# Biases of two projections from one group of two-column products, and a new order for the first two pairs of a four-layer transformer-like kernel

## The chip, the cores and the metric

The kernel runs on one core of a Trainium2 chip. The metric is the device time of one execution in microseconds (us), start to end. The engines are named as the profile names them: PE is TensorE (PEld its weight loads), DVE is VectorE, ACT is ScalarE, POOL is GpSimd, and SP is SyncE, which here only issues DMAs. All data is 32-bit floating point.

## The reference, cut to what matters

There are 32 samples; each has x and f (256 positions by 256 features). Four residual layers follow each other:

```python
x = x + attention(x, f, seq_len)      # 16 heads of 16; keys and values from x, one more from f itself
x = x + adapter(x, language_id)       # two small products, then a normalisation
x = x + (x @ W[subject].T + b[subject])
x = x + pool(x, prompt_type)          # tanh scores, masked softmax over positions
```

In the attention the queries and the keys have biases that are added to the inputs ahead of the projection:

```python
query = f + b_self
key   = concatenate([x + b_prev, f + b_self])
q = query @ Wq + bq
k = key @ Wk + bk
```

The kernel folds each of these into one bias per output feature, computed once: `b_self @ Wq + bq` for the queries, `b_prev @ Wk + bk` for the keys of x, and `b_self @ Wk + bk` for the keys of f.

## The kernel before, in words

The samples go through in 16 pairs. Every pair is cut into some 200 steps, each a small function that issues a few instructions on one or two engines. No loop nest sets the order: tables give every step of a pair a place (a number), places of pair p are shifted by 16 for each pair, all steps of all pairs are sorted by place, and the instructions are issued in that order. Engines run their own instructions strictly in that order; waits between engines are semaphores. One table (`SLOTS`) serves the pairs 2 to 13, so that the steps of three to four pairs interleave the same way again and again; `FIRST` and `SECOND` hold the places of the pairs 0 and 1, two more tables those of the last two pairs, and `ONCE` those of the setup steps. So the order can differ between two kernels in the start alone and be the same for the rest.

The steps that matter here, with their lines:

- **Idle products** (`setup_warm`, L1236): two products of a constant 128x256 tile into a PSUM tile that nobody reads. They keep PE running. `setup_warm(n)` for n from 0 to 4 are five groups of them.
- **Bias products** (`shifted`, L1246): four products of 128x128 weights with one column each. `setup_q` (tile bq_ps), `setup_k` (bk_ps) and `setup_ks` (bks_ps) each issue one such group, then a few tiny operations of DVE. They need `bcols_in` and the weights `wks` or `wqs`.
- **Projections** (`proj_q`, `proj_k`, `proj_ks`, L1542): four rows of PE in the trace each, into qps, kps and ksps; `proj_v` and `self_values` (L1409) into v_ps and vs_ps.
- **First scores** (`s1`, L1646): keys as the moving operand, so that `row_max` (L1659, DVE, into nmpad) can take the maximum over keys of four heads at a time. All s1 tiles but four share one PSUM buffer: the next s1 can't start until `row_max` of the one before has read it.
- **Second scores** (`s2`, L1757): the same products transposed, into one other PSUM buffer, which `exps` (L1769, ACT) empties. The next s2 waits for that.
- s1 and s2 use 32 rows of the PE array per head, and `g` says which half of the rows. An s1 and an s2 of different halves that are neighbours in the queue run side by side.
- `max_T` (nm_ps, L1677), `own` (own_ps, L1597), `av` (L1779), `vs`, `tw_ps` (L1448) and the other products fill the time between two s1.

In what follows s1(b,n,g) is the s1 step of sample b (b = 2 x pair + i).

Of the kernel before, what the change touches and what calls it, by code (L numbers as in the profile page):

```python
# [36 lines left out]
    (("setup_warm", 3), -134.4553),  # L37
    (("setup_heads",), -117.1977),
    (("setup_load", "wk"), -107.6222),
    (("setup_warm", 2), -106.4704),  # L40
    (("setup_warm", 4), -100.8478),
    (("setup_len",), -86.8814),
    (("setup_load", "wq"), -85.6382),
    (("setup_ks",), -80.858),
    (("setup_load", "lang"), -58.21),
    (("setup_warm", 1), -46.8993),
    (("setup_ones",), -45.2227),
    (("setup_k",), -44.8904),
    (("setup_load", "wv"), -39.5338),
    (("setup_load", "bo"), -39.016),  # L50
    (("setup_load", "subj"), -36.5512),
    (("setup_load", "wo"), -33.8195),
    (("setup_q",), -32.6784),
    (("setup_tw_load", 0), -28.6522),
    (("setup_warm", 0), -17.3426),
    (("setup_load", "ptype"), -16.0265),
    (("setup_xconst",), -14.8955),
    (("setup_mcol",), -4.8071),
    (("setup_load", "pw"), -2.9408),
    (("setup_tw_load", 1), -2.291),  # L60
    (("setup_tw_bias",), 3.0863),
    (("setup_tw", 0), 4.4234),
    (("setup_tw_load", 2), 6.8896),
    (("setup_tw", 1), 7.7073),
    (("setup_tw_load", 4), 10.7892),
    (("setup_tw", 2), 13.4697),
    (("setup_tw_load", 3), 15.8592),
    (("setup_tw", 3), 19.3226),
    (("setup_tw", 4), 20.7528),
    (("setup_tw_load", 5), 22.4043),  # L70
    (("setup_pool",), 22.7791),
    (("setup_tw", 5), 24.2208),
    (("setup_tw_load", 6), 26.6611),
    (("setup_tw", 6), 27.4389),
    (("setup_vbc",), 34.3784),
    (("setup_tw_load", 7), 37.2938),
    (("setup_tw", 7), 40.4841),
# [207 lines left out]
    (("load_T", "xT"), -71.3129),  # L285
    (("key_mask", 0), -56.3002),
    (("mask_keys", 0), -50.461),
    (("load_T", "fT"), -49.4222),
    (("key_mask", 1), -46.3901),
    (("proj_q", 0), -28.2207),  # L290
    (("q_out", 0), -19.4412),
    (("proj_ks", 0), -17.1577),
    (("spread_q", 0, 0), -17.0194),
    (("mask_keys", 1), -16.4653),
    (("proj_q", 1), -15.9679),
    (("load_x",), -15.7202),
    (("spread_q", 0, 1), -15.5783),
    (("ks_out", 0), -15.5433),
    (("q_out", 1), -14.7452),
    (("proj_k", 0), -10.9121),  # L300
    (("proj_ks", 1), -10.3247),
    (("k_out", 0, 0), -9.1406),
    (("ks_out", 1), -8.2877),
    (("proj_v", 0), -7.7128),
    (("k_out", 0, 1), -6.3829),
    (("v_out", 0), -4.6066),
    (("s1", 0, 0, 1), -2.8235),
    (("s1", 0, 0, 0), -0.5535),
    (("proj_k", 1), -0.4229),
    (("row_max", 0, 0, 0), 0.4669),  # L310
    (("row_max", 0, 0, 1), 0.884),
    (("k_out", 1, 1), 2.0272),
    (("s1", 0, 1, 0), 2.8899),
    (("row_max", 0, 1, 0), 3.0595),
    (("self_values", 0), 3.1147),
    (("s1", 0, 1, 1), 3.3786),
    (("k_out", 1, 0), 3.8795),
    (("s1", 0, 2, 0), 4.0777),
    (("row_max", 0, 2, 0), 4.1575),
    (("row_max", 0, 1, 1), 4.238),  # L320
    (("vs_blocks", 0), 4.4602),
    (("s1", 0, 3, 0), 5.238),
    (("s1", 0, 2, 1), 5.4565),
    (("row_max", 0, 3, 0), 6.7563),
    (("s1", 1, 0, 0), 6.76),
    (("row_max", 0, 2, 1), 7.3706),
    (("s1", 0, 3, 1), 7.4376),
    (("spread_q", 1, 1), 7.6485),
    (("row_max", 1, 0, 0), 7.661),
    (("own",), 9.3522),  # L330
    (("row_max", 0, 3, 1), 9.5492),
    (("s1", 1, 0, 1), 10.0423),
    (("row_max", 1, 0, 1), 10.3329),
    (("max_T", 0), 10.3569),
    (("ones_rows", 0), 10.3914),
    (("own_out",), 10.7488),
    (("spread_q", 1, 0), 10.7762),
    (("s1", 1, 1, 0), 11.3645),
    (("max_own", 0), 11.5999),
    (("own_exp", 0), 11.7836),  # L340
    (("row_max", 1, 1, 0), 11.8145),
    (("s1", 1, 1, 1), 12.1572),
    (("s2", 0, 0, 0), 12.2591),
    (("row_max", 1, 1, 1), 12.5264),
    (("s1", 1, 2, 0), 13.2568),
    (("row_max", 1, 2, 0), 13.3839),
    (("exps", 0, 0, 0), 13.4022),
    (("s2", 0, 0, 1), 13.4124),
    (("s1", 1, 2, 1), 13.5948),
    (("exps", 0, 0, 1), 13.714),  # L350
    (("own_blocks", 0), 13.8403),
    (("s2", 0, 1, 0), 13.983),
    (("x_bias",), 14.4585),
    (("exps", 0, 1, 0), 14.7727),
    (("row_max", 1, 2, 1), 15.4798),
    (("proj_v", 1), 15.4854),
    (("s1", 1, 3, 0), 15.5535),
    (("s2", 0, 1, 1), 15.7304),
    (("exps", 0, 1, 1), 15.7305),
    (("weighted", 0), 15.7581),  # L360
    (("row_max", 1, 3, 0), 16.0315),
    (("s1", 1, 3, 1), 16.9468),
    (("s2", 0, 2, 0), 16.9651),
    (("row_max", 1, 3, 1), 17.0407),
    (("av", 0, 0), 17.0447),
    (("av", 0, 1), 17.6199),
    (("exps", 0, 2, 0), 18.4377),
    (("av_blocks", 0, 0), 18.446),
    (("ones_rows", 1), 18.9042),
    (("v_out", 1), 18.968),  # L370
    (("sums", 0, 0), 18.9765),
    (("s2", 0, 2, 1), 18.9799),
    (("max_T", 1), 19.2223),
    (("exps", 0, 2, 1), 19.399),
    (("s2", 0, 3, 0), 19.8184),
    (("exps", 0, 3, 0), 19.8964),
    (("max_own", 1), 19.8964),
    (("av", 0, 2), 20.1287),
    (("s2", 0, 3, 1), 20.2874),
    (("exps", 0, 3, 1), 20.3348),  # L380
    (("own_exp", 1), 20.558),
    (("s2", 1, 0, 0), 21.0468),
    (("av", 0, 3), 21.6144),
    (("exps", 1, 0, 0), 21.7231),
    (("with_own", 0, 0), 21.8227),
    (("s2", 1, 0, 1), 22.1821),
    (("exps", 1, 0, 1), 22.2235),
    (("self_values", 1), 22.3238),
    (("av_blocks", 0, 1), 22.5492),
    (("vs_blocks", 1), 22.7345),  # L390
    (("s2", 1, 1, 0), 23.1936),
    (("sums", 0, 1), 23.6381),
    (("exps", 1, 1, 0), 23.8054),
    (("s2", 1, 1, 1), 23.9013),
    (("av", 1, 0), 24.0492),
    (("exps", 1, 1, 1), 24.5088),
    (("with_own", 0, 1), 24.7647),
    (("s2", 1, 2, 0), 25.0826),
    (("exps", 1, 2, 0), 25.1529),
    (("av", 1, 1), 25.3201),  # L400
    (("av_blocks", 1, 0), 25.5849),
    (("att_T", 0), 25.7719),
    (("s2", 1, 3, 0), 25.7801),
    (("own_blocks", 1), 25.8013),
    (("exps", 1, 3, 0), 26.1089),
    (("out_proj", 0), 26.2623),
    (("x1_out", 0), 26.4979),
    (("s2", 1, 2, 1), 26.5221),
    (("weighted", 1), 26.6676),
    (("exps", 1, 2, 1), 27.3647),  # L410
    (("load_adapter", 0), 27.443),
    (("blocks", 0, "x1"), 27.6156),
    (("s2", 1, 3, 1), 27.8925),
    (("av", 1, 2), 28.1614),
    (("exps", 1, 3, 1), 28.4053),
    (("av", 1, 3), 29.02),
    (("sums", 1, 0), 29.1336),
    (("with_own", 1, 0), 29.1947),
    (("av_blocks", 1, 1), 29.6903),
    (("load_adapter", 1), 29.7913),  # L420
    (("sums", 1, 1), 30.082),
    (("x1_b2", 0), 30.1782),
    (("with_own", 1, 1), 30.7119),
    (("to_dram", 0, "x1"), 30.7583),
    (("att_T", 1), 31.1704),
    (("load_pool",), 31.5326),
    (("out_proj", 1), 31.5501),
    (("x1_out", 1), 31.6749),
    (("x1_beta", 1), 31.6866),
    (("blocks", 1, "x1"), 31.7378),  # L430
    (("to_dram", 1, "x1"), 32.1915),
    (("from_dram", 0, "x1"), 32.74),
    (("from_dram", 1, "x1"), 33.1075),
    (("hidden",), 33.6373),
    (("x1_b2", 1), 34.2189),
    (("h_out",), 35.1321),
    (("adapted",), 35.3561),
    (("y_out", 1), 35.67),
    (("y_out", 0), 35.8418),
    (("norm_stats", 0), 36.4135),  # L440
    (("norm_rstd", 0), 36.4274),
    (("norm_stats", 1), 36.9029),
    (("norm_rstd", 1), 38.0777),
    (("norm_shift", 0), 38.1002),
    (("norm_shift", 1), 38.1822),
    (("norm", 1), 38.8884),
    (("x1_beta", 0), 39.4462),
    (("x2_out", 1), 39.4886),
    (("load_subject",), 40.5689),
    (("blocks", 1, "x2"), 41.1393),  # L450
    (("norm", 0), 41.7146),
    (("x2_out", 0), 42.754),
    (("to_dram", 1, "x2"), 44.1278),
# [637 lines left out]
def cond_resid_kernel(  # L1091
# [43 lines left out]
    def g_tile(name):  # L1135
        return ps_g.tile([P, 512], F32, tag="g", name=name)
# [1027 lines left out]
```

## Time and profile before

| | |
|---|---|
| median of 3 runs | 1030.31 us (1029.19 to 1030.33) |
| the profiled execution | 1031.86 us, its span from first to last instruction 1030.1 us |
| PE busy | 1017.4 us, 99% of the span |
| DVE, ACT, POOL busy | 77%, 50%, 36% |
| granted PE clock, mean over the span | 0.994 of full speed |

The span leaves 1.8 us around it. PE rows: one product of 32-bit data shows as two rows ("x8" is four products). Ends of PE rows are modelled and include the time in which a product drains, so that a busy PE is not a PE without pauses. The chain of work that ended last is better for pauses: it follows each instruction back to what released it.

### The profile page before, as it was taken

Reading aid. Unit: us, or ns where it says so; the run is one execution under the profiler, and the core shown is the slowest. Engines: PE = TensorE matmul, PEld = TensorE weight load, DVE = VectorE, ACT = ScalarE, POOL = GpSimd, SP = SyncE. Lnnn points to the kernel's source line nnn. Section 1 sums busy time; section 2 is a strip of 40 time slices with the busy share of each in tenths; the row PEclk is TensorE's granted clock in tenths of the full one; section 3 lists DMA queues with packets and bytes.
Section 4 is the critical chain, followed back from the end, with each engine's and each line's share of the span. In section 5 each row is a group of like instructions: output and inputs, shape, how many; then the busy total and the mean of one; then the engine's idle time right before and its main releaser. Section 6 shows DMA issues by size and latency. Waiting matters only on the chain.

```text
span 1030.1 us, 21215 instructions
## 1 busy us (share of the span) xinstructions
PE 1017.4 (99%) x7612; PEld 616.4 (60%) x7612; DVE 793.5 (77%) x1419; ACT 510.1 (50%) x798; POOL 366.1 (36%) x490
## 2 busy tenths in 40 slices
PE   9999999999999999999999999999999999999997
PEld 6466555665656656565665656556565665656565
DVE  4666686878878878787888878787887878877674
ACT  2344454546455555544645454455545455554552
POOL 3014334333334324343333334333333433342461
PEclk9999999999999999999999999999999999999999
DMA  4123334534656454464635536463454645445341
GB/s 172 28 70 113 84 113 124 135 102 113 175 121 171 99 136 126 101 165 118 169 92 136 142 95 171 115 170 88 131 161 107 150 113 143 117 107 129 81 116 61
DMA packets 205487, 125.18 MB, mean 122 GB/s; under 512 B 128646, under 2 KB 176518, under 8 KB 205382
## 3 DMA queue, kind: packets, MB, share of 16 engines
q1 hardware_dynamic: 204854, 122.25, 44.9%
q8 instruction: 60, 0.98, 0.4%
q10 hardware_dynamic: 288, 0.79, 0.2%
q0 software_dynamic: 240, 0.79, 0.2%
q14 instruction: 45, 0.37, 0.1%
HBM read 90.47 MB, written 31.73 MB: 119 GB/s over the span
## 4 chain that ended last, share of the span: by engine, by line
PE 97%; DVE 1%; ACT 1%; issue 1%; POOL 0%; DVEq 0%; ACTq 0%; POOLq 0%
PE s L1646 16%; PE s L1757 12%; PE av L1779 11%; PE qps L1542 6%; PE vs_ps L1409 6%; PE v_ps L1409 6%; PE o_ps L1409 6%; PE kps L1542 6%; PE p_ps L1409 6%; PE ksps L1542 6%; PE z_ps L1409 6%; PE y_ps L1890 2%; PE t_ps L1973 2%; PE h_ps L1864 2%; PE sc_ps L2001 1%; PE nm_ps L1677 1%
## 5 line engine op out<-in xcount | busy, mean ns | idle before, releaser
L1769 ACT ACTIVATE e<-s 128x1024 f32<-128x1024 f32 x256 | 261.5, 1023 | 329.7 <-PE s L1757 228.8
L1659 DVE TENSOR_REDUCE nmpad<-s 128x4 f32<-128x1024 f32 x256 | 310.4, 1214 | 93.8 <-PE s L1757 65.7
L1646 PE MATMUL s<-k,qc 32*128 32x512 f32 x1024 | 284.4, 639 | 2.1 <-DVE nmpad L1659 2.0
L1757 PE MATMUL s<-q,k 32*128 32x256 f32 x2048 | 285.6, 400 | 0.9 <-ACT e L1769 0.8
L1757 PEld LDWEIGHTS s<-q,k 32*128 32x128 f32 x2048 | 172.6, 184 | 23.7 <-ACT e L1769 8.1
L1646 PEld LDWEIGHTS s<-k,qc 32*128 32x128 f32 x1024 | 75.9, 183 | 117.3 <-issue 28.4
L1779 PE MATMUL av<-e,vpad 128*32 128x256 f32 x2048 | 130.5, 383 | 0.1
L1810 POOL TENSOR_TENSOR vs<-bt,vs 128x256 f32<-128x256 f32 x64 | 51.9, 811 | 208.3 <-DVE bt L1791 199.0
L1779 PEld LDWEIGHTS av<-e,vpad 128*32 128x32 f32 x2048 | 58.2, 109 | 58.8 <-issue 28.1
L1569 ACT ACTIVATE k<-kps,kbias,cols 128x512 f32<-128x512 f32 x64 | 46.8, 774 | 60.0 <-PE kps L1542 55.2
L1811 POOL TENSOR_TENSOR vs<-vs,zs 128x256 f32<-128x256 f32 x64 | 40.4, 631 | 96.3 <-DVE zs L1801 93.2
L1855 POOL TENSOR_TENSOR x1b<-x,an 128x512 f32<-128x512 f32 x32 | 40.7, 1273 | 80.5 <-DVE x L1834 75.1
L1542 PE MATMUL qps<-fT,wqs 128*128 128x512 f32 x128 | 65.1, 633 | 0.1
L1916 POOL TENSOR_SCALAR rstd<-mv 128x2 f32<-128x2 f32 x32 | 7.5, 235 | 162.0 <-DVE mv L1909 162.0
L1409 PE MATMUL p_ps<-x2b,prT 128*128 128x256 f32 x256 | 63.9, 394 | 0.4 <-DVE pz L2030 0.4
L1409 PE MATMUL v_ps<-wvs,xT 128*128 128x256 f32 x256 | 63.6, 391 | 0.6 <-ACT vpad L1622 0.6
L1409 PE MATMUL vs_ps<-fT,wvs 128*128 128x256 f32 x256 | 63.8, 392 | 0.0
L1409 PE MATMUL o_ps<-wos,attT 128*128 128x256 f32 x256 | 63.4, 390 | 0.0
L1409 PE MATMUL z_ps<-ws,x2T 128*128 128x256 f32 x256 | 62.5, 387 | 0.0
L1542 PE MATMUL kps<-xT,wks 128*128 128x512 f32 x128 | 62.3, 609 | 0.0
L1542 PE MATMUL ksps<-fT,wks 128*128 128x512 f32 x128 | 61.9, 606 | 0.0
L1409 PEld LDWEIGHTS p_ps<-x2b,prT 128*128 128x128 f32 x256 | 48.1, 194 | 17.2 <-issue 11.6
(138 smaller groups left out, 1461.2 us busy)
## 6 DMA issues: line engine op xcount, KB each, us to landing
an<-in_adn SPq DMA_DIRECT2D x32, 384.0 KB
mk<-pool_d SPq DMA_DIRECT2D x32, 257.0 KB
fT<-in_fT SPq DMA_DIRECT2D x16, 512.0 KB
xs<-in_x SPq DMA_DIRECT2D x32, 256.0 KB
ws<-in_swT SPq DMA_DIRECT2D x32, 256.0 KB
out<-x2b SPq DMA_DIRECT2D x32, 256.0 KB
xT<-in_xT SPq DMA_DIRECT2D x15, 512.0 KB
swap_d<-x1bl SPq DMA_DIRECT2D x112, 64.0 KB
```

Of the source, the lines that this page charges most:

```text
L1409: nc.tensor.matmul(ps[:, q, :n], lhsT=lhsT(c, q), rhs=rhs[:, c, :], start=(c == 0), stop=(c == 1),)
L1542: nc.tensor.matmul(ps, lhsT=w[:, ci, c * P : (c + 1) * P], rhs=T[src, p][:, ci].rearrange("p b s -> p (b s)"), start=(ci == 0), stop=(ci = ...
L1569: nc.scalar.activation(joint("k", p, work, [P, 2, 2, 2, S])[:, u, c].rearrange("p b s -> p (b s)"), T["kps", p, c], AF.Identity, bias=kbia ...
L1646: nc.tensor.matmul(ps[:, j].rearrange("p (u s) -> p u s", u=2), lhsT=T["qc", p][r, c, i, q * P : (q + 1) * P], rhs=T["k", p][r, :, c, i, : ...
L1659: nc.vector.tensor_reduce(nm_bufs[i][:, q, to : to + 8].rearrange("p (u j) -> p j u", u=2)[:, 2 * g : 2 * g + 2], T.pop(("s1", b, n, g)).r ...
L1757: nc.tensor.matmul(ps[:, j, k, :], lhsT=T["k", p][r, u, c, i, k * P : (k + 1) * P], rhs=T["q", p][r, u, c, i, :], start=True, stop=True,)
L1769: nc.scalar.activation(e, T.pop(("s2", b, n, g)), AF.Exp)
L1779: nc.tensor.matmul(ps[j * HB : (j + 1) * HB, u, :], lhsT=v_bufs[b % 3][:, k, 8 * c + 2 * j + u, :], rhs=e[j // 2][:, j % 2, k, :], start=( ...
L1810: nc.gpsimd.tensor_tensor(vs, bt[:, :, :, 0:DH], vs, ALU.add)
L1811: nc.gpsimd.tensor_tensor(vs, vs, z.unsqueeze(3).to_broadcast([P, S // HB, 2, DH]), ALU.mult)
L1855: nc.gpsimd.tensor_tensor(x1b, x1, bc_q(T["an", b][:, D : 2 * D]), ALU.add)
L1864: nc.tensor.matmul(ps[i * A : (i + 1) * A, :], lhsT=T["a1", b][:, c * A : (c + 1) * A], rhs=T["x1T", b][:, :, c], start=(c == 0), stop=(c ...
```

## The change

The biases of the keys of x and of f come from one group of products: `shifted` takes the columns straight out of `bcols_in` and multiplies the weights `wks` with two columns at a time; `setup_k` then does the additions of both. `setup_ks` is gone, and so is one of the five groups of idle products (n = 4). That leaves 6 products fewer in all: four of one column and two of 256 columns.

```diff
-    def shifted(w, shift, name):
-        b_ps = g_tile(name)
+    def shifted(w, first, n, name):
+        b_ps = g_tile(name)[:, 0 : 2 * n].rearrange("p (c n) -> p c n", n=n)
         for c in range(2):
             for ci in range(2):
                 nc.tensor.matmul(
-                    b_ps[:, c : c + 1],
+                    b_ps[:, c, :],
                     lhsT=w[:, ci, c * P : (c + 1) * P],
-                    rhs=shift[:, ci : ci + 1],
+                    rhs=bcols_in[:, first + ci : first + ci + 2 * n - 1 : 2],
...
     def setup_k():
-        ps = shifted(wks, bps, "bk_ps")
-        nc.vector.tensor_tensor(bcol[:, 2:4], ps[:, 0:2], bks, ALU.add)
+        ps = shifted(wks, 6, 2, "bk_ps")
+        nc.vector.tensor_tensor(bcol[:, 2:4], ps[:, :, 0], bks, ALU.add)
+        nc.vector.tensor_tensor(bcol[:, 4:6], ps[:, :, 1], bks, ALU.add)
...
-    def setup_ks():
-        ps = shifted(wks, bss, "bks_ps")
-        nc.vector.tensor_tensor(bcol[:, 4:6], ps[:, 0:2], bks, ALU.add)
```

The tables `ONCE`, `FIRST` and `SECOND` have new places throughout; `SLOTS` and those of the last two pairs are as they were. The places of the setup's products, for instance:

```diff
-    (("setup_warm", 3), -134.4553),
-    (("setup_warm", 2), -106.4704),
-    (("setup_warm", 4), -100.8478),
-    (("setup_ks",), -80.858),
-    (("setup_warm", 1), -46.8993),
-    (("setup_k",), -44.8904),
-    (("setup_q",), -32.6784),
-    (("setup_warm", 0), -17.3426),
+    (("setup_warm", 3), -127.8016),
+    (("setup_warm", 2), -113.4772),
+    (("setup_k",), -45.375),
+    (("setup_q",), -43.1653),
+    (("setup_warm", 1), -39.98),
+    (("setup_warm", 0), -34.8564),
```

What this makes of PE's queue in the built programs, at the four places of which more is said below (products, in order; brackets hold neighbours that are both s1 or s2):

```
start, before: warm3 warm2 warm4 bks warm1 bk bq qps(0,0) warm0 ksps(0,0) qps(0,1) xc kps(0,0) ksps(0,1) v(0)
start, after:  warm3 warm2 bk bq warm1 warm0 qps(0,0) qps(0,1) ksps(0,0) kps(0,0) xc ksps(0,1) v(0)

pair 0, before: s1(0,3,1) tw own s1(1,0,1) nm s1(1,1,0) qps(1,0)
pair 0, after:  tw s1(1,0,1) own nm s1(1,1,0) qps(1,0)

pair 1, before: vs(4) [s1(3,2,0) s2(2,0,1)] v(3) [s1(3,2,1) s2(2,1,0)] kps
pair 1, after:  vs(4) [s1(3,2,0) s2(2,0,1) s1(3,2,1) s2(2,1,0)] kps

later, before: av(3) s2(3,2,1) nm [s1(5,1,0) s2(3,3,0)] qps
later, after:  nm av(3) [s2(3,2,1) s1(5,1,0) s2(3,3,0)] qps
```

SP's queue has the same DMAs in a new order: the first eight are the same, then the output weights come ahead of the value weights, and both halves of the first x ahead of the first subject weights.

## The prediction, as it was made before the run

> **What bounds the kernel now.** I read the page's busy times first, then its chain of waits, then the chain in order of time for the first 120 us, and last the busy time of PE in stretches of 3.41 us. The page:
>
> ```profile
> PE 1017.4 (99%) x7612; PEld 616.4 (60%) x7612; DVE 793.5 (77%) x1419; ACT 510.1 (50%) x798; POOL 366.1 (36%) x490
> PE 97%; DVE 1%; ACT 1%; issue 1%; POOL 0%; DVEq 0%; ACTq 0%; POOLq 0%
> ```
>
> PE is the bound, and from 150 to 854 us it is busy in every stretch of 64 us without a pause. The tables of the pairs 2 to 13 are untouched, so this stretch keeps its length if the first two pairs hand it the same work. The change is decided in the first 150 us: by what stands in PE's queue there, by pauses, and by the granted clock. The chain in order of time (start, us, what), from the idle products to the first projection:
>
> ```profile
> 2.42 5.42 PE warm L1236 x12
> 7.84 0.83 PE bks_ps L1246 x8
> 8.67 0.97 PE warm L1236 x4
> 9.64 0.80 PE bk_ps L1246 x8
> 10.44 0.03 issue
> 10.47 1.16 PE bq_ps L1246 x8
> 11.63 0.10 issue
> 11.73 3.39 PE qps L1542 x4
> 15.12 0.86 PE warm L1236 x4
> ```
>
> Four rows of idle products take 5.42 x 4/12 = 1.8 us in the first line and 0.86 us in the last; qps takes 3.39 us here and 1.72 us at 17.70. So PE runs at half speed until about 7.8 us and again at 11.7. Later, in pair 0:
>
> ```profile
> 42.95 0.02 issue
> 42.97 1.24 DVE nmpad L1659
> 44.21 0.04 issue
> 44.25 1.13 PE s L1646 x4
> 45.38 3.61 PE qps L1542 x4
> ```
>
> An s1 waits 1.30 us for `row_max` of the s1 before it with nothing but a 0.22 us transpose to fill, and the projection after it takes 3.61 us instead of the 1.91 us of the next one (at 50.06). The stretches of 3.41 us say why (us; then PE, PEld, DVE, ACT and POOL busy; granted clock; DMA):
>
> ```profile
> 7.80:11.21 3.41, 3.36 (x28) 3.20 (x26) 2.36 (x10) 0.00 (x0) 0.28 (x1) 1.00 0.78 279
> 11.21:14.62 3.41, 3.31 (x7) 1.71 (x7) 1.63 (x5) 0.00 (x0) 1.41 (x2) 0.50 0.79 282
> 41.93:45.34 3.41, 2.45 (x11) 0.70 (x11) 3.14 (x5) 0.99 (x2) 0.00 (x0) 1.00 0.28 58
> 45.34:48.76 3.42, 3.42 (x6) 1.14 (x4) 1.23 (x1) 0.42 (x1) 0.00 (x0) 0.50 0.14 50
> 52.17:55.59 3.42, 3.15 (x33) 2.30 (x29) 1.88 (x5) 1.34 (x2) 0.59 (x2) 1.00 0.05 15
> ```
>
> The stretch of bias products (7.80) and the one with the 0.96 us pause (41.93, busy 2.45) are followed by a stretch at half clock; the one with a 0.27 us pause (52.17) is not. One-column products count as busy in the row, but evidently not for the clock. A half-clock stretch costs 3.41 / 2 = 1.7 us.
>
> **Part 1, the start.** bks (0.83), the group of idle products at 8.67 (0.97) and part of the others stand where PE would wait anyway. bq needs the query weights; POOL waits until 9.71 us for the x of pair 1, which SP issued (1.67 us) just ahead of these weights (2.15 us), and bq ran at 10.47. So the weights land between about 9.7 and 10.47; I take 10.4. Removing bks and one idle group therefore gains at most 0.7 us, and I count nothing. A group of two-column products shows in no row; one column took 0.80 to 0.83 us, 64 columns (tw_ps at 94.76) 0.84 us. It lies under the same load: nothing.
>
> What counts is the path from bq to the end of qps(0,0). Before: 10.47 to 15.98 us with qps and one idle group behind it. After, two idle groups stand ahead of qps and none behind, and each waits for the one before to drain (rows last 0.38 us at a spacing of 0.22, so about 0.2 us each, twice). The price goes by the clock. The stretch 7.80 to 11.21 holds only 0.8 us of bk and the first 0.8 us of bq, less than before, so half clock from 11.21 is near certain if the stretches lie as they did. bq at half clock takes 2 x 0.80 = 1.6 us and ends at 12.05. The two idle groups need 3.6 us at half clock; 2.57 us are done at 14.62, the rest goes at full speed in 0.5 us: 15.1. With 0.4 us of draining and 1.72 us for qps: 17.2 us, against 15.98: **+1.2 us**. Bounds: with full clock from 11.21 us, 11.65 + 2 x 0.86 + 0.4 + 1.72 = 15.5: -0.5. With half clock until 18.04: the idle groups end at 12.05 + 3.6 + 0.4 = 16.05, qps has 1.0 of its 1.72 us done at 18.04 and ends at 18.8: +2.8.
>
> **Part 2, the order up to the fourth pair.** Up to the first s1 of sample 8 both queues hold the same groups, among them 64 s1 and 53 s2. A run of neighbours costs 0.42 + 0.22 + 0.21 + 0.22 = 1.07 us (chain at 60.52 us) whether it is one group or an s1 with an s2 beside it. Counted in the two queues, 63 runs become 62: -1.07 us. Two of the 62 are chains of four and of three groups, which save a change of the tiles' shape each (0.2 us: v_ps costs 1.92 behind an s and 1.73 behind a 128-row product): -0.4.
>
> Pauses that shrink: own (0.57 us) moves between s1(1,0,1) and s1(1,1,0) and fills most of the 0.96 us: -0.6. s1(0,3,1) now stands beside s1(1,0,0) instead of after it: -0.6. Three s1 of sample 2, between 67 and 74 us, are released by `row_max` in the chain (69.72, 72.17) and now have ksps, v or av in front: 0.3 to 0.4 each, -1.1. New pauses: s1(3,2,1) follows s1(3,2,0) with only an s2 beside it, near 105 us: +1.3, the whole row of 42.95. s2(3,3,0) waits for `exps` of s2(3,2,1) with only an s1 beside it, near 150 us: 1.02 us of `exps` and its semaphores: +1.0. Two s1 near 31 and 35 us: +0.7. A few of 0.1 to 0.25: +0.5. Together +3.5 - 2.3 = +1.2. Part 2 is -1.07 - 0.4 + 1.2 = -0.3; uncertain by the small pauses, each read off a queue and not off a row: from -1.3 to +0.7.
>
> What is late next where a pause goes: PE itself, the next product is ready. SP's new order brings no wait that I can find: output weights, value weights and x are issued from 6.4 us on and needed from 20 us; the row copies that s2 waits for are issued behind the same `max_own` and land 1.6 us later. Cover for the subject weights: tw_ps needs them from 36 us, 20 us after issue.
>
> **Part 3, the clock behind the pauses.** The pause at 43 us shrinks to about 0.4 us, near the 0.27 us that left the clock alone: -1.7 us. Each of the two new pauses can bring a half-clock stretch, +1.7, if enough of it lies inside one stretch; a pause of 1.3 us lies whole in one with (3.41 - 1.3) / 3.41 = 0.6. I take one of the two: +1.7; bounds 0 and +3.4.
>
> The Trainium skill, "TensorE: Matmul & The Clock Gate", Part 1 ("HAM oscillation"), says that the clock falls only after pauses of more than about 3.4 us. The row of 41.93 us contradicts it: 0.96 us of pause were enough. By the page the new pauses would not touch the clock, and the sum below would be 1.7 us smaller. The same part calls the window free-running, so that its place changes from run to run; the stretches here are 3.41 us long as it says, but one trace can't show whether they move.
>
> **Sum.** +1.2 - 0.3 - 1.7 + 1.7 = +0.9 us on the span of 1030.1. The profiled execution took 1031.86 us, the median of the runs 1030.31; I take the difference to that median: **1031.2 us**. Differences under 0.2% (2.06 us) are what a measurement of this kernel can't tell from none.
>
> **Rivals.** *Slower: the idle groups don't wake the clock.* Place: 11.21 to 14.62 us, which after the change holds 0.85 us of one-column products and 2.57 us of idle ones, 75% of it; before, the same stretch held 2.9 us of real products (85%) and full clock followed; the one at 41.93 held 72% by its row and half clock followed. If 75% is too little, part 1 is +2.8: 2.8 - 0.3 - 1.7 + 1.7 = +2.5, 1032.8 us. It decides from about three quarters of a stretch. Chance 0.22. *Slower by the pauses:* both new pauses lie whole in a stretch: 1.2 - 0.3 - 1.7 + 3.4 = +2.6, 1032.9 us; chance 0.14. *Faster:* the stretches lie otherwise in time, the idle groups run at full clock and neither new pause catches a stretch: -0.5 - 0.3 - 1.7 = -2.5, 1027.8 us; chance 0.17. It needs two things at once, but the smaller queue speaks for it. *The change takes away nothing that counts:* the removed products all lay under loads, and the rest cancels within 1 us; this is within my forecast, whose chance is 0.47.
>
> **How the numbers follow.** Faster 0.17, same 0.47, slower 0.22 + 0.14 = 0.36. The range reaches down to -2.1, which takes in the near side of the faster rival, and up past both slower ones, to +3.6 (half clock until 18.04 and part of one more stretch): 1028.2 to 1033.9. Left out are the far side of the faster rival and both slower mechanisms at once (+4.2).
>
> **What would show it.** Right: bq starts near 10.4 us with PE idle before it; the two idle groups lie between bq and qps at 0.43 us a row; qps(0,0) ends near 17 us; qps of pair 1 takes 1.9 us instead of 3.61; pauses of 1.3 and 1.0 us near 105 and 150 us, one of them followed by a stretch at clock 0.50. Wrong: qps(0,0) ending by 15.5 or after 18.5 us; no pause near 105 us; or any new pause between 170 and 854 us, where I expect none.

## The result and the profile after

The changed kernel takes 1032.87 us (median of 20 runs, 1030.57 to 1035.24) against 1030.3 us (20 runs, 1028.57 to 1033.02): a ratio of 1.0022, 95% interval [1.0016, 1.0029], or 2.3 us more (the two medians lie 2.6 us apart). That is just over the 0.2% that the forecast took for no change. The forecast was 0.9 us more, and its range holds the time. The profiled execution took 1033.33 us, with a span of 1031.5 us against 1030.1.

From the page, busy times of the engines and the chain by engine:

```profile
PE 1013.3 (98%) x7600; PEld 614.2 (60%) x7600; DVE 796.8 (77%) x1419; ACT 509.1 (49%) x798; POOL 365.4 (35%) x490
PE 96%; DVE 2%; DMA 1%; issue 1%; ACT 0%; POOL 0%; SPq 0%; DVEq 0%; POOLq 0%; ACTq 0%
```

PE has 12 instructions fewer (the eight of bks, four of the idle group) and is busy for 4.1 us less, but the span is 1.4 us longer: PE now waits for 18.2 us rather than 12.7. The chain in order of time shows where (start, us, what). The start:

```profile
2.13 8.13 DMA wqs<-in_wq
...
10.40 1.84 PE bq_ps L1245 x8
12.24 1.93 PE warm L1234 x4
...
14.21 1.85 PE warm L1234 x4
...
16.11 3.70 PE qps L1539 x8
...
27.55 1.07 PE s L1643 x8
```

bq starts at 10.40 us and the two idle groups lie between it and the projections, as forecast, but each takes 1.9 us for four rows, not 0.86: nearly all of it, up to 15.68 us, is at half clock. Stretches of 3.41 us (us; then PE, PEld, DVE, ACT and POOL busy; granted clock; DMA):

```profile
5.44:8.85 3.41, 1.44 (x10) 0.97 (x8) 1.02 (x4) 0.00 (x0) 1.28 (x2) 1.00 1.02 411
8.85:12.26 3.41, 1.86 (x9) 1.89 (x10) 0.72 (x5) 0.00 (x0) 0.19 (x1) 0.50 0.79 257
12.26:15.68 3.42, 3.36 (x8) 2.17 (x8) 2.34 (x7) 0.00 (x0) 1.40 (x2) 0.50 0.96 313
15.68:19.09 3.41, 3.35 (x9) 1.44 (x8) 0.00 (x0) 0.92 (x2) 0.00 (x0) 1.00 0.42 150
```

Two stretches run at 0.50, one behind the other; before, one did. They begin at 5.44 + 3.41 k here and at 7.80 + 3.41 k there: the stretches do move from one execution to the next. The idle groups do wake the clock (the stretch that they fill, 12.26, is followed by 1.00), but they run at half clock themselves. The first s1 of pair 0 starts at 27.55 us; before it was 25.44.

The qps of pair 1, and the pauses that the forecast named, in the chain in order of time:

```profile
46.92 1.91 PE qps L1539 x4
...
106.13 1.24 DVE nmpad L1656
...
107.41 0.56 PE s L1643
...
150.30 1.03 ACT e L1766
...
151.38 1.13 PE s L1754 x8
152.51 1.92 PE qps L1539 x4
```

Both pauses are there with the forecast lengths. The qps behind the second takes 1.92 us, and no stretch near 106 or 150 us is at 0.50. The qps of pair 1 at 46.92 us takes 1.91 us instead of 3.61: the half-clock stretch at 45 us is gone. One pause is new that was not named: at 212.53 us stands a z_ps, ahead of which PE waits 0.40 us (the profile names DVE). In the profile of before PE has no pause between 150 and 854 us.

### The profile page after: what moved, and what is told of

The parts are those of the page before. It is cut to its first block, busy times and chain, and to the rows that moved or that the text cites. A ratio compares the mean times of both kernels' runs of the same rounds, so it can differ in the third digit from the quotient of the medians.

```text
span 1031.5 us, 21196 instructions
## 1 busy us (share of the span) xinstructions
PE 1013.3 (98%) x7600; PEld 614.2 (60%) x7600; DVE 796.8 (77%) x1419; ACT 509.1 (49%) x798; POOL 365.4 (35%) x490
## 3 DMA queue, kind: packets, MB, share of 16 engines
q1 hardware_dynamic: 204854, 122.25, 44.5%
## 4 chain that ended last, share of the span: by engine, by line
PE 96%; DVE 2%; DMA 1%; issue 1%; ACT 0%; POOL 0%; SPq 0%; DVEq 0%; POOLq 0%; ACTq 0%
PE s L1643 16%; PE s L1754 12%; PE av L1776 12%; PE vs_ps L1406 6%; PE o_ps L1406 6%; PE kps L1539 6%; PE v_ps L1406 6%; PE ksps L1539 6%; PE p_ps L1406 6%; PE z_ps L1406 6%; PE qps L1539 5%; PE y_ps L1887 2%; PE t_ps L1970 2%; PE h_ps L1861 2%; PE sc_ps L1998 1%; PE nm_ps L1674 1%
## 5 line engine op out<-in xcount | busy, mean ns | idle before, releaser
L1539 PE MATMUL qps<-fT,wqs 128*128 128x512 f32 x128 | 61.9, 607 | 0.1
```

Source lines behind the costliest of these rows:

```text
L1539: nc.tensor.matmul(ps, lhsT=w[:, ci, c * P : (c + 1) * P], rhs=T[src, p][:, ci].rearrange("p b s -> p (b s)"), start=(ci == 0), stop=(ci = ...
```

## The experiments

Ratios are to the kernel before, on the same chip, with 95% intervals; 0.001 of it is 1.03 us. The places are those of the tables ONCE, FIRST, SECOND and SLOTS. First the change was taken apart on the queue of before, one piece more each time.

**code_only.** The new `setup_k` with the two-column group; of the tables only this:

```
-    (("setup_warm", 4), -100.8478),
-    (("setup_ks",), -80.858),
```

> The shared two-column group and one idle group fewer, with the order of before's queue kept (bk in the place that it had, bks and the fifth idle group gone). Theory of the prediction: what is removed lay under the load of the query weights, so the time is that of before within 0.5 us (ratio 0.9995 to 1.0005), bq still starts near 10.4 us and qps(0,0) still ends near 16 us; the 2.6 us by which the changed kernel is slower then come from the new order alone. Rival: the removal itself changes the clock at the start, PE being idle for longer before bq; then it is 1.7 us (one stretch at half clock) slower, ratio 1.0016, and qps(0,0) ends near 17.7 us.

1.0004 [0.9995, 1.0013]. The shared group and the missing idle group together measure +0.4 us, with an interval of -0.5 to +1.3: what the change is named for does nothing to the time that these runs can show. What the rival describes does occur in the profiled execution: half clock lasts from 11.03 to 17.85 us, two stretches where the profile of before has one, and the first s1 starts at 27.00 rather than 25.44 us. The median does not show its 1.7 us.

**start_only.** The same, and the two last idle groups go behind bq:

```
-    (("setup_warm", 1), -46.8993),
+    (("setup_warm", 1), -31.0),
+    (("setup_warm", 0), -30.0),
-    (("setup_warm", 0), -17.3426),
```

> The kernel before with the shared two-column group, one idle group fewer, and only one piece of the new order: two idle groups stand between bq and qps(0,0), and none between qps(0,0) and the next projection. Theory: this is the start as the changed kernel has it, and it costs the 2.1 us by which v(0) ended later there (27.55 against 25.44 us); ratio 1.0020, and the rest of the new order then costs 0.5 us in all. Rival: the idle groups would have been run anyway and only change places, so the start costs at most one drain, 0.4 us (1.0004), and the 2.1 us come from the other order of the projections and loads after it.

1.0045 [1.0031, 1.0058]: 4.2 us more than code_only and 4.6 us more than before, twice the theory's 2.1 us and far over the rival's 0.4. The first s1 starts at 27.59 us, as late as in the changed kernel. The executions profiled with before's order at the start (code_only without one idle group and bks) have it at 25.44 (before), 27.00 (code_only), 23.98 (own_moved, below), 25.64 and 23.98 us (pause_each and pause_filled, below), 25.2 us in the mean. Those with the new start have it at 27.55 (after), 27.59 (start_only), 27.48 (start_own) and 28.57 us (av_into_pause), 27.8 in the mean. So the start itself is worth about 2.6 us, by few executions that spread over 3.0 us in the first group, and the rest of the 4.2, some 1.6 us, would have come later. The stretches of start_only around 43 us show where it can come from:

```profile
43.02:46.44 3.42, 2.46 (x20) 0.98 (x19) 2.87 (x6) 0.99 (x2) 0.00 (x0) 1.00 0.09 25
46.44:49.85 3.41, 3.41 (x6) 1.30 (x7) 2.16 (x4) 0.42 (x1) 0.00 (x0) 0.50 0.24 83
49.85:53.26 3.41, 3.41 (x13) 1.30 (x13) 0.00 (x0) 0.69 (x1) 0.00 (x0) 0.50 0.02 5
```

In this execution the old pause before s1(1,1,0) brings two stretches at half clock, where the profile of before had one.

**start_own.** start_only, and own goes into that pause, as the changed kernel has it:

```
-    (("own",), 9.3522),
+    (("own",), 10.7),
```

> The kernel with the shared group and the two idle groups behind bq on the queue of before, and own moved behind s1(1,0,1) as in the changed kernel. Theory: own's move is what the rest of the new order gives back, 1.4 to 2.6 us of the 4.6 that the start costs: ratio 1.0018 to 1.0031, near the changed kernel's 1.0022. Rival: other changes of the order (fewer runs of neighbours, smaller pauses in pair 1) give it back, and own alone only 0.5 us: 1.0038 to 1.0045.

1.0012 [1.0003, 1.0021]: 3.4 us less than start_only, with intervals that don't meet. From the first s1 to s1(1,1,0) the two profiles differ by 0.24 us only (27.48 to 46.05 against 27.59 to 46.40). The rest is the clock: s1(1,1,0) and the qps behind it take 1.13 and 1.91 us in the chain of start_own, and 2.08 and 3.71 us in that of start_only.

**own_moved.** The same edit on the kernel before, alone.

> The kernel before with one move: own (the product of 0.57 us of pair 0) goes from ahead of s1(1,0,1) to behind it, into the pause of 0.96 us before s1(1,1,0). Theory: it fills the pause (0.5 us less) and the stretch at half clock behind it, in which the projection took 3.61 instead of 1.91 us, goes too (1.7 us less): 2.2 us faster in all, ratio 0.9979. Rival: the half-clock stretch has another cause (the narrow products of s1 that fill the stretch before it, whose rows use half of the array), so only the 0.5 us go, ratio 0.9995. Second rival: the half-clock stretch comes in some executions only, and the gain of the medians lies between.

1028.10 us, 0.9986 [0.9967, 1.0005]. The interval is too wide to part the theories. Eight of eleven runs took 1026.6 to 1029.1 us and three 1032.6 to 1035.5, with mean granted clocks of 0.998 to 0.999 and of 0.992 to 0.993. In its profile no stretch between the first record at 6.59 us and 1023 us is at half clock.

Then the changed kernel was mended, one piece at a time.

**idle_early.** The two last idle groups go ahead of bk:

```
-    (("setup_warm", 1), -39.98),
-    (("setup_warm", 0), -34.8564),
+    (("setup_warm", 1), -113.4),
+    (("setup_warm", 0), -113.3),
```

> The changed kernel with its two last idle groups moved from behind bq to ahead of bk, where PE waits for weights. Theory A, the idle groups are on the path and do nothing for the clock: qps(0,0) starts at about 12.2 us rather than 16.1 us, at half clock, and ends near 15.5 us rather than 18 us: 2 to 2.5 us faster than the changed kernel, about the time of before (0.9997 to 1.0005 of it). Rival B, they are what brings the full clock: without them two more stretches run at half clock, and of the 3.9 us that they took all but about 0.5 us is lost again; ratio 1.0018 to 1.0025.

0.9985 [0.9974, 0.9996], 1028.90 us: 3.8 us less than the changed kernel, more than theory A asked. In its profile bq is done under the load of f, which is the last of these loads to end, at 11.53 us; the first two qps start at 11.67 us and end at 17.03, against 16.11 and 19.81 in the changed kernel.

**no_idle.** The two groups are left out.

> The changed kernel without its last two idle groups (the two of 2.4 us at the start stay). Theory, the idle groups behind bq only stand on the path: the same time as with them ahead of bk, 0.9985 of before, within 0.0007. Rival, four idle groups are needed to bring the full clock early: two leave more executions at half clock until about 15 us, which costs one stretch of 1.7 us in part of them; ratio 0.9993 to 1.0005.

1.0000 [0.9991, 1.0009]: 2.3 us less than the changed kernel, so behind bq they cost more than they bring. It is about 1.5 us more than idle_early, as the rival foretold, though the two intervals overlap a little.

**idle_between.** The two groups go behind bk (places -44.5 and -44.45), into the wait for the query weights.

> The changed kernel with its last two idle groups between bk and bq, in the time in which PE waits for the query weights. Theory, only the place behind bq costs: they lie under the load whether the clock is full (1.7 us) or half (3.6 us, of which up to 1 us is left over); ratio 0.9985 to 0.9993 of before. Rival, two idle groups cost their own time wherever they stand after 8 us: 1.0015 to 1.0022, as the changed kernel.

0.9995 [0.9981, 1.0009], which doesn't part the two. The chain of its profile tells more:

```profile
7.25 1.84 PE bk_ps L1245 x8
9.08 3.62 PE warm L1234 x8
12.71 1.50 PE bq_ps L1245 x8
14.20 5.27 PE qps L1539 x8
```

Every row there up to 17.55 us is at half clock, and the first record of the clock is of 17.55 us. Until a first record the clock column shows 1.00, so only the durations tell: in this execution PE ran at half speed from the first idle product, at 2.4 us, to 17.55 us. The two groups at 2.4 us last 3.6 us, and were not enough.

**av_into_pause.** One product of pair 0 goes into the pause near 105 us:

```
-    (("av", 1, 3), 29.7296),
+    (("av", 1, 3), 30.25),
```

> The changed kernel with one av of pair 0 (eight products, 1.07 us) moved into its new pause near 105 us, between s1(3,2,0) and s1(3,2,1). Theory: the pause falls from 1.31 to about 0.3 us and, in the executions in which it brings a stretch at half clock, that goes too: 1.0 us less in all executions and up to 1.7 us more in some, ratio 0.9996 to 1.0012 of before. Rival: the av is now late for the output product behind it, which waits in its place; ratio 1.0018 to 1.0026, no change.

1.0009 [1.0000, 1.0019]: 1.3 us less than the changed kernel, with an uncertainty of 1.2 us: about what the pause lost, and no sign of a half-clock stretch beside it. In the table of waits of PE the longest wait of an s1 for `row_max` falls from 1.3 to 0.4 us.

**both_closed_early.** idle_early, av_into_pause, and s2(3,3,0) behind the qps that followed it:

```
-    (("s2", 1, 3, 0), 26.8634),
+    (("s2", 1, 3, 0), 27.292),
-    (("s2", 1, 3, 1), 27.2971),
+    (("s2", 1, 3, 1), 27.78),
```

(with their `exps` at 27.5 and 27.79).

> A candidate: the changed kernel with the two idle groups ahead of bk, an av in the pause near 105 us, and the product of the query behind s2(3,2,1) ahead of s2(3,3,0), so that the pause near 150 us is closed too. If the parts add: 0.9985 of before from the idle groups, 1.0 us and 1.0 us from the pauses, 0.5 to 1.5 us from the clock behind them: ratio 0.9950 to 0.9962, about 1026 us. Rival: with the start earlier the loads bound the first products, or new waits stand behind the moved products; ratio 0.9975 to 0.9990.

1025.87 us, 0.9957 [0.9944, 0.9970]. The parts add: 2.9 us less than idle_early for the two pauses (with an uncertainty of 1.8), and 4.4 us less than the kernel before.

**closed_6_idle.** The same, and two more idle groups between bk and bq (places -44.9 and -44.8).

> The candidate with both pauses closed, and two more groups of idle products between bk and bq, where PE waits for the query weights: six groups in all, none behind bq. Theory: four early groups bring the full clock by about 8 us and the two in the wait keep it, so the stretches at half clock that lay over the first two projections go in most executions: 1 to 2.5 us faster than the candidate, ratio 0.9933 to 0.9948 of before. Rival: PE is at half clock there and the two groups push bq back by 1 to 2 us, or the clock falls in the projections' wait anyway: 0.9957 to 0.9975.

1025.13 us, 0.9945 [0.9932, 0.9958]. This is the fastest of all, but the interval reaches over that of both_closed_early. Its start, and the stretches there:

```profile
2.42 6.57 PE warm L1236 x16
...
9.78 1.83 PE warm L1236 x8
...
12.40 3.54 PE qps L1541 x8
```

```profile
8.30:11.71 3.41, 3.41 (x23) 3.12 (x22) 1.24 (x6) 0.00 (x0) 0.18 (x1) 1.00 0.81 296
11.71:15.13 3.42, 3.42 (x14) 1.97 (x14) 2.37 (x7) 0.83 (x2) 0.78 (x1) 1.00 0.84 245
```

bq starts at 11.62 us, 1.2 us later than in the changed kernel, and the first two qps still end at 15.94 rather than 19.81 us, all at full clock.

Last, the disputed price of a pause was measured by itself.

**pause_each.** The kernel before, with the pause of 105 us in each of the pairs 2 to 13:

```
-    (("s1", 1, 2, 1), 13.774),
-    (("s2", 0, 1, 0), 13.7971),
+    (("s1", 1, 2, 1), 13.12),
+    (("s2", 0, 1, 0), 13.122),
```

> The kernel before with one more pause in each of the pairs 2 to 13: s1(1,2,1) with the s2 beside it stands directly behind s1(1,2,0), as the changed kernel has it once near 105 us, so PE waits 1.3 to 2 us for row_max twelve times. Theory: a pause of this length brings a stretch at half clock (3.41 us at 0.50) in 4 to 8 of the twelve, as the prediction reckoned with 0.6 of them; 12 x 1.5 us of pauses and 6 x 1.7 us of clock, about 28 us. Rival: such pauses leave the clock alone, as those of 106 and 150 us in the profile of the changed kernel did: no stretch at 0.50 between 150 and 850 us, 18 us in all.

1.0172 [1.0156, 1.0188], 17.7 us: the rival's 18 us. In the table of waits of PE (total, times, longest):

```profile
PE s L1646 <- DVE nmpad L1659: 19.6, 17, 1.5
```

That is 17.6 us over before's 2.0. No stretch between 150 and 850 us is at 0.50, and the mean granted clocks of the four runs, 0.994 to 0.998, are those of before. Two stretches with a pause, each with the one behind it:

```profile
42.83:46.24 3.41, 2.45 (x10) 0.99 (x9) 3.05 (x6) 0.71 (x2) 0.00 (x0) 1.00 0.29 99
46.24:49.65 3.41, 3.41 (x18) 1.56 (x17) 1.67 (x2) 1.65 (x3) 0.00 (x0) 1.00 0.03 7
285.18:288.59 3.41, 1.88 (x20) 1.27 (x15) 2.87 (x5) 2.95 (x7) 1.89 (x3) 1.00 0.41 67
288.59:292.00 3.41, 3.41 (x17) 2.91 (x16) 2.23 (x7) 1.77 (x5) 1.78 (x1) 1.00 0.52 126
```

A stretch in which PE is busy for 1.88 us leaves the clock alone. The first pair is the old pause at 43 us: busy for 2.45 us, as in the stretch at 41.93 us of before that half clock followed, and here full clock follows. So PE's busy time alone does not decide.

**pause_filled.** The same, with a group of idle products ahead of the moved s1 in each pair:

```
+    (("keep_warm", 9), 13.115),
```

> The kernel with the twelve pauses, and a group of idle products (0.86 us) in each, so that PE is busy but no further. Theory that the clock falls by the pause: the same delay by row_max with pauses of at most 1 us, and no or few stretches at half clock; 5 to 10 us less than without the filling. Rival, the pauses alone cost and the clock does not count: the time without the filling within 2 us, since the product behind the pause is released at the same moment.

1.0155 [1.0139, 1.0171], within 2 us of pause_each, the rival again: the delay by `row_max` costs the same whether PE stands still in it or runs idle products. The waits for `row_max` fall to 7.0 us, the time hardly. The only stretch at half clock in the profile before 1026 us is one at 43.90 us, behind the old pause.

## Why the prediction was nearly right, point by point

Its sum came out 1.4 us too low. The miss at the start was twice that in the medians, and misses the other way (own's move gained 1.1 us more than forecast, less than its uncertainty, and no half-clock stretch was seen behind the new pauses) took half of it back: that the sum came so near is luck in part. The runs give a sum of their own: the code +0.4 us, the idle groups behind bq +4.2, own into the pause -3.4, and the rest of the order +1.0 (the changed kernel's 1.0022 against start_own's 1.0012). Each has an uncertainty of 0.9 to 1.7 us. If the profiles stand for the other runs, some 1.6 us of the second term is clock behind the pause at 43 us, which the third takes away again; without that the two are about +2.6 and -1.8.

- **The removed products cost nothing: right** within the interval of code_only, -0.5 to +1.3 us.
- **Part 1, the start: the term that was off.** It was +1.2 with bounds of -0.5 and +2.8. The first s1 came 2.1 us later in the profile of after than in that of before, and 2.6 us later in the mean of four and five profiled executions; in the medians start_only measured +4.2, and idle_early gave 3.8 back on the new queue. What failed is the condition "if the stretches lie as they did": it took their boundaries from one execution (7.80 and 11.21 us). With the new start the first record lies at 5.30, 5.44, 5.48 and 18.07 us; three of these executions show two stretches at half clock in a row, and in the fourth every row until 18 us is at half speed. So the idle groups ran at half clock nearly to their end (3.87 us in the profile of after, where the sum had 3.45), and in the fourth qps(0,0) did in part, too. One thing was missing in the sum: with two groups ahead of bk instead of four, PE idles before bk and bq (in the profile of after it is busy for 1.44 us of the stretch at 5.44), and the clock is lost earlier or not won at all. no_idle and idle_early, which differ by two such groups, are 1.5 us apart. The end of bq, 12.05 us in the sum and 12.24 us in the profile, was right by luck: the sum priced all of bq at half clock, but its own half-clock stretch began only at 11.21 us, when a bq of 0.80 us from 10.4 us on is done. It ran at half clock because the clock had fallen at 8.85 us already.
- **The named checks.** bq at 10.4 us with PE idle before it, the new pauses at 106 and 150 us, and the qps of pair 1 at 1.91 us: all seen. The first qps ends near 18 us (16.11 plus half of 3.70) instead of 17, within the bounds. Two are wrong: no pause is followed by clock 0.50, and where no new pause was expected, from 170 to 854 us, there is the one of 0.40 us ahead of the z_ps at 212.53 us. Its cause was not tested; it is small beside the other terms.
- **Part 2, the order.** The pause near 105 us was put at +1.3 and measured 1.3 (av_into_pause); both together +2.3, and closing both gave 2.9. Right, within uncertainties of 1.2 and 1.8 us. The gains by shorter runs and by small pauses were not measured alone. What the sum of the runs leaves for them, +1.0 less 2.3 to 2.9, is near the forecast's -2.0, but has an uncertainty of more than 1 us.
- **Part 3, the clock.** The -1.7 behind the pause at 43 us was right in kind: own's move, forecast at -0.6 and -1.7, measured -3.4 on the new start and -1.4 on the old, there with an interval of -3.4 to +0.5. The size varies because the half-clock stretch does not come in every execution, and is doubled in some. The +1.7 for the new pauses was wrong: none of twelve such pauses changed the clock in the profile of pause_each, though six of them lie whole in one stretch (PE busy for 1.88 or 1.89 us of it). "Enough of it lies inside one stretch" was the faulty measure.
- **The Trainium skill** ("TensorE: Matmul & The Clock Gate", Part 1, "HAM oscillation") was put aside for the row of 41.93 us. For the new pauses it was the better guide, and the sum that it gave, 1.7 us lower, would have been too low for another reason, the start. For the pause at 43 us it stays wrong: the 0.96 us brought half clock in three of the five profiled executions in which it was left as it was (before, start_only, pause_filled; not in pause_each, nor in code_only, where a boundary of the stretches, at 45.16 us, parts the pause). Its free-running window is what the moving boundaries show.
- **The rivals.** "The idle groups don't wake the clock" gave 1032.8 us, nearest to the measured time, by a mechanism that is half right: in three profiles they wake it, but late enough that they run at half clock, and in the fourth half clock lasts until 18.07 us, as that rival has it.

What stays open is what the clock does count. The stretches 41.93 (before), 43.02 (start_only) and 40.48 us (pause_filled) hold s1 without an s2 beside them, transposes and at most 0.05 us of a projection (the one of start_only also own and half of a tw); the one at 42.83 us (pause_each), just as busy, holds 0.7 us of qps, and the one at 285.18 us holds s1 with s2 beside them (which take no longer than one alone) and 0.4 us of a 128-row product. That fits a count by how much of the array is in use.

An estimate from the fourteen traces points the same way. Take 0.214 us for every 256 columns that a PE row streams at full clock (the spacing of the idle rows), twice that at half clock, times the share of the 128x128 array that its rows and columns use, and add this up for each stretch of 3.41 us behind a first clock record. The 25 full-clock stretches that half clock followed hold at most 1.23 us of it. Of the 4139 that full clock followed, all but three hold 1.25 us or more; the three, at 1007 to 1012 us, hold 1.07 or 1.08. The stretch at 41.93 us of before holds 1.04, the one at 42.83 us of pause_each 1.34, and the six that hold one of its new pauses whole 1.29 to 1.45: by this estimate these pauses left the clock alone by a narrow margin. A half-clock stretch was followed by full clock from 2.67 us on (17 of them) and by half clock up to 2.66 (7). This was reckoned afterwards; no run varied the use of the array alone.

## What to carry to other kernels

Where idle products are to wake the clock, put them where PE waits for its first weights, as many as last until these come (the fastest kernel here does so, though its interval reaches over the next one's), and none on the path between the last load and the first real product. Price such a group at half clock (1.9 us here), and work out the start for several positions of the stretches: one profile shows one of them. A pause in the middle of a dense stretch costs its own length; it is worth moving work into it first where the neighbours are narrow products, since the clock can fall there.

## What was not expected of the hardware

- Equal busy times of PE, 2.45 to 2.46 us of 3.41, were followed by half clock in three executions and by full clock in another, and 1.88 us by full clock.
- The executions of one kernel differ by whole half-clock stretches: the runs of before that the experiments share lie mostly about 1028.7, 1030.3 and 1031.7 us, with mean granted clocks of 0.998, 0.997 and 0.994 to 0.995, in steps of about 1.5 us. Not all of these stretches lie where the change is: five of the fourteen profiles, before and after among them, have one that begins about 19 us ahead of the end, the others none there. An effect of 1 us is seen only in medians over many runs.
- PE can stay at half speed until 18 us with two idle groups ahead of its loads, while the clock column shows 1.00 for want of a record.
